# A four-layer decoder on one core: layer 0's expert output normalised inside the next attention, early router logits, ordered expert lists, a new pace of side work, and early loads for layer 2

## The chip, the cores and the metric

The kernel runs on one core of one Trainium2 chip. The metric is device time in microseconds for one execution of the whole decoder; less is better. Engines are named as in the profile: PE (matmuls), PEld (its weight loads), DVE, ACT, POOL, and SP, which issues most DMAs. L12 is line 12 of the kernel before.

## The reference, cut to what matters

The decoder works on x of 16 sequences × 100 positions × 128 features, with a context of 1444 × 96 for each sequence. Twelve sublayers follow one another, each added to x: four layers of attention, cross-attention and a feed-forward part. Those that the change touches compute:

```python
# layer 0, cross-attention: 16 heads over the 1444 context rows
# layer 0, feed-forward: the two best of 8 experts
probs = softmax(x @ gate_w.T + gate_b); w, idx = top_k(probs, 2); w = w / w.sum(-1)
y = sum over the two experts e of  w_e * (silu(x @ w1[e]) * (x @ w3[e])) @ w2[e]
# layer 1, attention: 16 heads of 8, weights quantised to 5 levels; softmax of masked scores
# layer 2, attention: batch norm, two softmaxes per head, difference, root mean square per head
att = softmax(q1 @ k1) - lam * softmax(q2 @ k2); y = rms_norm(att @ v) * (1 - lam0); x = x + y @ c
# layer 2, cross-attention: 16 heads over the context
# layer 3, cross-attention: softmax over the 32 largest scores only, then an S4D convolution and a small MLP
# layer 3, feed-forward: the two best of 8 experts, softmax over the two logits
```

Every sublayer normalises x over its 128 features first. All arithmetic of x is in f32.

## The kernel before, in words

x lies in SBUF as X, 100 partitions (positions) × 16 batch elements × 128 features. It is worked on in NG = 4 groups of four batch elements. Before a sublayer, each group's rows get statistics (`stats4`, L335: bn_stats and bn_aggr on DVE, the power −0.5 on POOL in `root`, L354 and L356), are normalised into XN (`norm4`, L345, four DVE operations at L348), and turned by PE into XT, features on partitions (four transposes in `ahead`, L332, copied out at L292). `ahead` is a generator with three steps of this kind (statistics and root, XN, turn), and `at_once` runs all three. Sublayers run `ahead` for the next one group by group where they can.

A scheduler sets the order of each engine's instructions from the program's order and its own estimates; instructions wrapped in `pin` or `keep_in_program_order` keep the order in which they are written.

**Layer 0's cross-attention** (`l0_xattn`) runs 64 units of a batch element and four heads, 12 context chunks each, on a step counter `d` from 0 to 11. Steps 7 and 10 advance `ahead` of the group that has just ended. **Layer 0's experts** (`moe`, L1519) begin with the router: `logits` (L1334) is a product per batch element into one PSUM tile and one DVE add; `exps`, `top2` and `share` follow on DVE. `route` then builds, for 32 tiles of 128 (token, expert) places, the lists of rows: one-hot tables r_th, r_tv (L1460), r_oh (L1463) and r_tw (L1501) on DVE, sums on PE, and at the end the integers r_ti (source rows, L1489) and r_di (destination rows, L1491). For each of the 32 tiles POOL gathers rows by an indirect DMA (L1554), PE turns them (L1559), makes two products of four 128×128 blocks each (L1575), DVE multiplies (L1579), PE makes the down product (L1585), ACT scales, and POOL scatters the rows to `yd` in HBM (L1589). Beside the tiles runs `side`: `s4d_rest`, which prepares the S4D kernel of layer 3 on DVE (its last twenty steps are a multiplication at L1874 and a reduction at L1875 each), and `quant`, which quantises layer 1's weights. Four steps of `side` are taken per tile. At the end both result rows are loaded back (yy), added to X (L1623), and with `follow` the groups are normalised and turned at once, all four, before layer 1's attention begins.

**The attention helper** (`attn`, L365) is shared. Its units are pipelined by hand over a loop: scores of unit i, the largest score on DVE (L414), the scores minus it on POOL (L415, 100×1600), the exponent on ACT (L419), transposes (L378, copied at L428), products with V, and row sums, up to eight units behind. POOL also makes kb for each unit (L388, 128×1600). `prep(g)` yields the projections of group g: group 0 runs ahead of the loop, the others one step per unit. A list `later` holds work of ended groups, advanced by one step per unit. `spread` (L486) makes the tile va and sets it to 1.0 on POOL (L489). **Layer 1's attention** has 16 units.

**Layer 2's attention** (`l2_attn`) has 32 units, two per batch element. Its `room` is a large tile of 12288 columns, of which 6400 hold queries and keys. When a group of four batch elements has ended, `ended(g)` goes to `later`: the square root on ACT (L721, with a table load), a reciprocal, four times o on POOL (L727), its transposes ps_ot, a copy on ACT (L734), the product ps_out and the addition to X (L740), then `ahead`: some 15 steps for a group. The list is chained, and what remains after the loop is run to its end. **Layer 2's cross-attention** (`l2_xattn`) loads its two weight tiles (L1122) and the context of batch elements 0 and 1 (L1136, L1137) through SP when it starts; its first matmuls are ps_q (from XT) and ps_k (from the context).

**Layer 3's thresholds** (`l3_means`) take, for each of 52 blocks of scores, the 32 largest of every row: maxima of segments (L1954), four rounds of max and replace (L1958, L1963) into `m8`, a slice of one tile `big` for all blocks, the mask wk on DVE (L1964), and its product with the exponents on POOL (L1971). At the end the 32nd largest of every block is read from `big`.

Of the kernel before, what the change touches and what calls it, by code (L numbers as in the profile page):

```python
# [221 lines left out]
class Decoder:  # L222
    def __init__(self, tc, ctx, ins, at, out):
# [45 lines left out]
        self.a_rs = cp.tile([S, B], F32, name="a_rs")  # L269
        self.bst = cp.tile([128, NG, 6], F32, name="bst")  # L270
# [95 lines left out]
    def attn(self, pools, units, halves, mode, finish, prep):  # L366
# [96 lines left out]
        for i in range(N + 8):  # L463
            at = lambda lag, step, *a: step(i - lag, *a) if 0 <= i - lag < N else None
            at(4, results)
            at(-1, masked)
            for g in range(4):
                at(0, scores, g)
                at(2, turned, g)
                if g == 0:  # L470
                    at(5, lambda j: next(fin[j], None))
                if g == 1:
                    at(6, lambda j: next(fin[j], None))
                    at(7, lambda j: next(fin[j], None))
                if g == 2:
                    at(1, numerators)
            at(0, maxima)
            at(3, values)
            at(4, lambda j: next(fin[j], None))
            if later:  # L480
                next(later[0], None)
            for p in preps[: i + 1]:
                next(p, None)
# [140 lines left out]
    def l1_attn(self):  # L624
        with ExitStack() as st:
# [5 lines left out]
            def prep(g):  # L631
                self.project(psT, g, self.w("l1_qkv", 0, 128), qT, None, 1.0 / math.sqrt(8.0))
# [6 lines left out]
    def l2_attn(self):  # L639
        nc = self.nc  # L640
        with ExitStack() as st:
# [7 lines left out]
            room = self.fw.tile([128, 12288], F32, tag="big", name="l2_qk")  # L649
            t = [room[:, j * NT : (j + 1) * NT] for j in range(4)]  # L650
# [303 lines left out]
    def l0_xattn(self):  # L954
# [9 lines left out]
        with ExitStack() as st:  # L964
# [101 lines left out]
            for s in range(NCH * (NU + 1) + LEAD + 6):  # L1066
# [23 lines left out]
                if d in (7, 10) and ahead:  # L1090
                    next(ahead[0] if d < 10 else ahead.pop(), None)
# [5 lines left out]
    def l2_xattn(self):  # L1097
# [13 lines left out]
        with ExitStack() as st:  # L1111
# [7 lines left out]
            def weights(tag, rows):  # L1119
                n = ins[tag].shape[-1]  # L1120
                t = xw.tile([rows, n], F32, name=f"{tag}_sb")
                nc.sync.dma_start(out=t, in_=ins[tag])  # L1122
                return lambda k: t[:, self.xat[tag][k][0] : sum(self.xat[tag][k])]
# [15 lines left out]
            fetch(0)  # L1139
            fetch(1)  # L1140
# [202 lines left out]

    def exps(self, lg, ne, w1):
# [62 lines left out]
    def route(self, sel, both, cmb, mc, w1, psM, psO):  # L1407
# [3 lines left out]
        nc = self.nc  # L1411
        ones = w1.tile([S, S], F32, name="ones")
# [25 lines left out]
        for j, v in enumerate((rk, cmb)):  # L1438
# [5 lines left out]
        nc.vector.tensor_scalar(hi, pos, 1.0 / 128.0, -127.0 / 256.0, ALU.mult, ALU.add)  # L1444
        nc.vector.tensor_scalar(hi, hi, RND, None, ALU.add)
        nc.vector.tensor_scalar(hi, hi, -RND, None, ALU.add)
        lo = w1.tile([S, 2 * B], F32, name="r_lo")
        nc.vector.scalar_tensor_tensor(lo, hi, -128.0, pos, ALU.mult, ALU.add)
        va = w1.tile([S, 2, 2 * B], F32, name="r_va")
        nc.vector.scalar_tensor_tensor(va[:, 0], hi, -2.0, mc("id64")[:S], ALU.mult, ALU.add)  # L1450
        nc.vector.tensor_tensor(va[:, 1], mc("id1")[:S], lo, ALU.subtract)
# [5 lines left out]
        nc.vector.tensor_tensor(th, mc("iota")[:S, :NTL].unsqueeze(1).to_broadcast([S, 2 * B, NTL]),  # L1457
                                hi.unsqueeze(2).to_broadcast([S, 2 * B, NTL]), ALU.is_equal)
        for j in range(2):
            nc.vector.tensor_tensor(tv[:, :, j], th, va[:, j].unsqueeze(2).to_broadcast([S, 2 * B, NTL]), ALU.mult)  # L1460
        pl = psO.tile([128, 512], F32, tag="po", name="ps_l")
        for i in range(0, 2 * B, 8):
            nc.vector.tensor_tensor(oh[:, i : i + 8], mc("iota")[:S].unsqueeze(1).to_broadcast([S, 8, 128]),  # L1463
                                    lo[:, i : i + 8].unsqueeze(2).to_broadcast([S, 8, 128]), ALU.is_equal)
# [17 lines left out]
        nc.vector.scalar_tensor_tensor(dst, lst[:, :NTL], 64.0, lst[:, NTL:], ALU.mult, ALU.add)  # L1482
        nc.vector.tensor_tensor(dst, dst, mc("own"), ALU.add)
        nc.vector.tensor_scalar(dst, dst, 0.0, 2.0 * NT + 128.0 * NTL - 1.0, ALU.max, ALU.min)
        tok = w1.tile([128, NTL], F32, name="r_tok")
        nc.vector.tensor_scalar(tok, dst, float(NT), -float(NT), ALU.is_ge, ALU.mult)
        nc.vector.tensor_tensor(tok, dst, tok, ALU.add)
        ti = w1.tile([128, NTL], I32, name="r_ti")
        nc.vector.tensor_scalar(ti, tok, NT - 1.0, None, ALU.min)  # L1489
        di = w1.tile([128, NTL], I32, name="r_di")  # L1490
        nc.vector.tensor_copy(di, dst)  # L1491

        def weights():
# [4 lines left out]
            for j in range(3):  # L1498
                nc.vector.tensor_copy(pb[:, j], cur)
                nc.vector.tensor_copy(pt[:, j], pb[:, j])  # L1500
                nc.vector.tensor_tensor(tw[:, :, j], th, pt[:, j].unsqueeze(2).to_broadcast([S, 2 * B, NTL]), ALU.mult)  # L1501
# [17 lines left out]
    def moe(self, wt, gw, bg, on_probs, follow, taps=False):  # L1519
# [4 lines left out]
        with ExitStack() as st:  # L1524
# [11 lines left out]
            lg = self.logits(gw, 8, bg, w1, psM)  # L1536
# [61 lines left out]
            for t in range(NTL):  # L1598
# [11 lines left out]
                for _ in range(4):  # L1610
# [4 lines left out]
            for g in range(NG):  # L1615
# [8 lines left out]
                if follow:  # L1624
                    self.at_once(g, psM)
# [252 lines left out]
    def l3_means(self, CT, odd, room, wqk, cq, aside=None):  # L1878
# [6 lines left out]
        with ExitStack() as st:  # L1885
# [21 lines left out]
            if fast:  # L1907
                big = xw.tile([128, NUN, 4, 8], F32, name="big")
# [37 lines left out]
            def candidates(s, ex, i):  # L1946
# [5 lines left out]
                m8 = big[:, i]  # L1952
# [11 lines left out]
                pin(nc.vector.tensor_scalar(wk, s, m8[:, 3, 7:8], None, ALU.is_ge))  # L1964
                yield wk, m8, nm
# [119 lines left out]
            if fast:  # L2085

                sure = xw.tile([128, NUN], F32, name="sure")
                nc.vector.tensor_scalar(sure, big[:, :, 3, 7], -0.5 * BIG, None, ALU.is_gt)
# [171 lines left out]
    def run(self, layers):  # L2260
# [4 lines left out]
        if 2 in layers:  # L2265
            self.moe(self.big("l0f"), self.w("l0_gw"), self.r("l0_bg"), True, True, taps=True)
# [16 lines left out]
        if 11 in layers:  # L2283
            self.moe(self.big("l3f"), self.w("l3_gw"), self.r("l3_bg"), False, False)
# [25 lines left out]
```

## Time and profile before

| | us |
|---|---|
| median of 3 runs | 4224.94 |
| lowest and highest | 4224.86, 4239.69 |
| the profiled execution | 4216.78 |
| its span in the profile | 4215.0 |
| PE, DVE, ACT, POOL busy | 3776.6 (90%), 2941.8 (70%), 2001.1 (47%), 1056.5 (25%) |
| layer 0's cross-attention ends, about | 1446 |
| first and last tile's POOL transfer of layer 0's experts | 1480.83, 1602.44 |
| first projection of layer 1's attention | 1631.68 |
| layer 2's attention: first units, last row sums | 2008, 2293 |
| first keys of layer 2's cross-attention (ps_k) | 2341.47 |
| layer 3's experts: logits, last matmuls of the tiles, about | 4070, 4173 |

Times inside the program are microseconds from the span's start. A row of groups reads: line, engine, operation, output<-input, shapes and count, then busy time and mean nanoseconds of one, then the idle time of the engine just before them and what ended it. A row of waits reads: waiting engine, tile and line, the releaser, then total, number and longest wait. The granted clock is TensorE's, 1.00 being full speed; over the whole execution it was 0.93.

### The profile page before, as it was taken

To read this page: it belongs to the slowest core of one execution; us is meant where nothing else is said; L and a number is where in the kernel's file an instruction comes from. 1 tells how busy PE (TensorE), PEld (TensorE's weight loads), DVE (VectorE), ACT (ScalarE), POOL (GpSimd) and SP (SyncE) were. 2 spreads that over 40 slices of the span, in tenths; PEclk is the share of its full clock that TensorE was granted. 3 is DMA by queue.
4 is the path that set the end of the run, shared out by engine and by line. 5 is a ranking of instruction groups with operands and counts; after the bars stand their busy time and mean duration, and the time that the engine had idled before them with its cause. 6 is when DMAs were issued, how large, how long until landed. Compare 5 with 4: busy or idle time off the path is not lost. (4 is left out here: it accounts for less than half of the span.)

```text
span 4215.0 us, 65293 instructions
## 1 busy us (share of the span) xinstructions
PE 3776.6 (90%) x24498; PEld 2419.7 (57%) x24498; DVE 2941.8 (70%) x7850; ACT 2001.1 (47%) x3941; POOL 1056.5 (25%) x755
## 2 busy tenths in 40 slices
PE   7899999999999877898998799999997978888658
PEld 4555555555555475574666365556665646666448
DVE  8677777777777775754675577666764678996744
ACT  3365666656666432332454254445453445665114
POOL 6400000000000055504785000000004445443125
PEclk9899999999999888999998799999998979998879
DMA  2200000000000010153000000000000011110012
GB/s 68 88 12 17 17 14 17 17 14 17 17 14 6 5 34 25 40 155 64 1 1 2 20 13 16 12 12 12 12 2 1 1 49 39 40 34 19 2 73 60
DMA packets 36883, 112.00 MB, mean 27 GB/s; under 512 B 4998, under 2 KB 19628, under 8 KB 35472
## 3 DMA queue, kind: packets, MB, share of 16 engines
q1 hardware_dynamic: 28786, 97.19, 8.0%
q0 software_dynamic: 4096, 8.40, 0.7%
q8 instruction: 197, 3.23, 0.3%
q10 hardware_dynamic: 3678, 2.16, 0.2%
q14 instruction: 126, 1.03, 0.1%
HBM read 100.97 MB, written 6.75 MB: 26 GB/s over the span
## 5 line engine op out<-in xcount | busy, mean ns | idle before, releaser
L971 PE MATMUL ps_s<-qk,ct 97*128 97x400 f32 (+1 forms) x1536 | 651.7, 507 | 0.7 <-DVE qk L999 0.7
L971 PE MATMUL ps_o<-st,cn 128*97 128x400 f32 (+1 forms) x1536 | 649.6, 505 | 0.0
L1216 DVE TENSOR_REDUCE pm<-ps_s 100x1 f32<-100x484 f32 (+1 forms) x768 | 469.0, 653 | 232.2 <-PE ps_s L1130 219.4
L1006 ACT COPY st<-ps_s 128x400 f32<-128x400 f32 (+1 forms) x768 | 375.8, 489 | 424.5 <-PE ps_s L971 421.6
L1251 ACT ACTIVATE pt<-ps_st 121x400 f32<-121x400 f32 (+1 forms) x768 | 343.9, 501 | 347.0 <-PE ps_s L1130 338.6
L1015 DVE TENSOR_TENSOR mx<-mx,st 128x400 f32<-128x400 f32 (+1 forms) x640 | 365.0, 570 | 165.4 <-ACT st L1006 163.1
L1130 PE MATMUL ps_s<-K,q 32*100 32x484 f32 (+1 forms) x1536 | 421.8, 630 | 1.7 <-DVE pm L1216 1.6
L1036 DVE TENSOR_TENSOR st<-st,nb 128x400 f32<-128x400 f32 (+1 forms) x768 | 402.9, 566 | 8.6 <-ACT nb L1032 2.5
L971 PEld LDWEIGHTS ps_s<-qk,ct 97*128 97x128 f32 (+1 forms) x1536 | 267.0, 184 | 233.5 <-issue 92.2
L1037 ACT ACTIVATE st<-st 128x400 f32<-128x400 f32 (+1 forms) x768 | 378.0, 535 | 42.3 <-DVE st L1036 41.9
L1130 PE MATMUL ps_st<-q,K 32*121 32x300 f32 (+3 forms) x3072 | 380.3, 365 | 0.6 <-ACT pt L1251 0.6
L971 PEld LDWEIGHTS ps_o<-st,cn 128*97 128x97 f32 (+1 forms) x1536 | 237.2, 163 | 233.6 <-issue 142.8
L1025 POOL TENSOR_TENSOR nd<-cst_sb,nm 100x400 f32<-100x400 f32 x64 | 54.7, 854 | 1139.8 <-DVE nm L1023 1139.8
L1130 PEld LDWEIGHTS ps_st<-q,K 32*121 32x121 f32 (+1 forms) x3072 | 272.4, 182 | 47.5 <-issue 4.8
L354 POOL TENSOR_SCALAR a_rs<-a_mv 100x4 f32<-100x4 f32 x60 | 14.0, 234 | 980.4 <-DVE a_mv L340 973.0
L378 PEld LDWEIGHTS ps_pt<-cst_sb,sc 100*100 100x100 f32 x1280 | 138.8, 131 | 135.1 <-issue 88.7
L1937 PE MATMUL ps_s<-ct,qk 97*128 97x512 f32 (+3 forms) x384 | 173.8, 668 | 46.5 <-ACT sc L1943 36.1
L2015 PEld LDWEIGHTS ps_m<-rw,l3x_ex 128*128 128x128 f32 (+1 forms) x1536 | 192.7, 203 | 37.4 <-POOL rw L2007 27.0
L1971 POOL TENSOR_TENSOR l3x_ex<-l3x_ex,wk 128x1444 f32<-128x1444 f32 x52 | 168.6, 3243 | 179.3 <-DVE wk L1964 91.8
L2015 PE MATMUL ps_m<-rw,l3x_ex 128*128 128x100 f32 (+1 forms) x1536 | 198.7, 288 | 16.5 <-POOL rw L2007 16.3
L415 POOL TENSOR_TENSOR sc<-sc,mx 100x1600 f32<-100x1600 f32 x64 | 183.2, 2863 | 107.8 <-DVE mx L414 82.3
L1954 DVE MAX8 cd<-sc 128x8 f32<-128x45 f32 (+1 forms) x1664 | 182.4, 189 | 22.0 <-ACT sc L1943 21.9
(538 smaller groups left out, 7057.4 us busy)
## 6 DMA issues: line engine op xcount, KB each, us to landing
ct<-in_ctxT SPq DMA_DIRECT2D x64, 541.5 KB
cn<-in_ctxn SPq DMA_DIRECT2D x48, 582.0 KB
wb<-gd SPq DMA_DIRECT2D x8, 800.0 KB
l0f_sb<-in_l0f SPq DMA_DIRECT2D x3, 2048.0 KB
l3f_sb<-in_l3f SPq DMA_DIRECT2D x3, 2048.0 KB
wts_sb<-in_wts SPq DMA_DIRECT2D x1, 2320.0 KB
l0x_raw<-in_l0x SPq DMA_DIRECT2D x1, 1800.0 KB
l1f_sb<-in_l1f SPq DMA_DIRECT2D x1, 1728.0 KB
```

What stands on the lines that cost most here:

```text
L415: pin(nc.gpsimd.tensor_tensor(scs[i], scs[i], mx.unsqueeze(2).to_broadcast([S, NH, S]), ALU.subtract))
L971: mm = lambda *a, **k: tc.keep_in_program_order(nc.tensor.matmul(*a, **k))
L1006: nc.scalar.copy(t[:n], ps[:n, :G4])
L1015: nc.vector.tensor_tensor(MX[u][:n], MX[u][:n], t[:n], ALU.max)
L1036: nc.vector.tensor_tensor(t[:n], t[:n], NM[u][:n], ALU.subtract)
L1037: nc.scalar.activation(t[:n], t[:n], AF.Exp)
L1130: mm = lambda *a, **k: tc.keep_in_program_order(nc.tensor.matmul(*a, **k))
L1216: nc.vector.tensor_reduce(pm[:, a, r // 32, n : n + 1], ps[:S, : n1 - n0], AX.X, ALU.max)
L1251: nc.scalar.activation(pt[: n1 - n0, r // 32, :], ps[: n1 - n0, :G4], AF.Exp)
L1937: nc.tensor.matmul(o, lhsT=q, rhs=ctx[bb][:, n0:n1], start=True, stop=True)
L1954: pin(nc.vector.max(cd[:, k, :], s[:, n0:n1]))
L2015: nc.tensor.matmul(acc[b][:, c // 4, (c % 4) * S : (c % 4 + 1) * S], lhsT=ex[r0:r1, c * 128 : (c + 1) * 128], rhs=rw[r0:r1], start=first a ...
```

## The change

Seven edits. (1) `moe` no longer normalises and turns its output: `prep(g)` of layer 1's attention does it, in its first two steps. (2) The router's logits are made per group by a new `logits4` into a tile that lives through the program; in layer 0 groups 0 to 2 are done inside the cross-attention, in a step `d == 11` to which the turn of `ahead` moves from step 10; `moe` does the rest (`known` groups are left out). Layer 3 makes all four in `moe`. (3) In `route`, the DVE instructions from r_hi to r_di, with r_tw, are pinned in program order, in both expert layers. (4) `side` gets two steps per tile. (5) `later` gets two steps per unit. (6) `l2_attn` issues the loads of layer 2's cross-attention weights and of the context of batch elements 0 and 1 into the unused columns of `room`. (7) In `l3_means`, `m8` is a rotating tile, and its last column is copied by POOL into a small tile `last`, once for each of 52 blocks.

```diff
 # attn
-            if later:
-                next(later[0], None)
+            for p in later[:1] * 2:
+                next(p, None)
...
 # l1_attn
             def prep(g):
+                steps = self.ahead(g, psT)
+                next(steps)
+                yield
+                next(steps)
+                next(steps, None)
+                yield
                 self.project(psT, g, self.w("l1_qkv", 0, 128), qT, None, 1.0 / math.sqrt(8.0))
...
 # l2_attn
             room = self.fw.tile([128, 12288], F32, tag="big", name="l2_qk")
+            self.early, p = {}, 4 * NT
+            for tag, rows in (("l2x", 128), ("l2xk", CA), (0, CA), (1, CA)):
+                n = CK if tag in (0, 1) else self.ins[tag].shape[-1]
+                e = self.early[tag] = room[:rows, p : p + n]
+                nc.sync.dma_start(out=e, in_=self.ins["ctxT"][tag] if tag in (0, 1) else self.ins[tag])
+                p += n
...
 # l0_xattn
                 if d in (7, 10) and ahead:
-                    next(ahead[0] if d < 10 else ahead.pop(), None)
+                    next(ahead[0], None)
+                if d == 11 and ahead and 0 <= v < NU - 1:
+                    next(ahead.pop(), None)
+                    self.logits4(v // (4 * NQ), self.w("l0_gw"), self.r("l0_bg"), psA)
...
 # l2_xattn
-                t = xw.tile([rows, n], F32, name=f"{tag}_sb")
-                nc.sync.dma_start(out=t, in_=ins[tag])
+                t = self.early[tag]
...
-            fetch(0)
-            fetch(1)
+            cts.update({b: self.early[b] for b in range(2)})
...
+    def logits4(self, g, gw, bias, psp):
+        ps = psp.tile([128, 512], F32, tag="ps", name="ps_lg")
+        for j in range(4):
+            b = 4 * g + j
+            self.nc.tensor.matmul(ps[:S, 8 * j : 8 * j + 8], lhsT=self.XT[:, b * S : (b + 1) * S], rhs=gw,
+                                  start=True, stop=True)
+        self.nc.vector.tensor_tensor(self.lg[:, 4 * g : 4 * g + 4, :], ps[:S, :32].rearrange("p (b e) -> p b e", e=8),
+                                     bias.unsqueeze(1).to_broadcast([S, 4, 8]), ALU.add)
...
 # route: pin(...) around each DVE instruction from r_hi to r_di, r_tw among them
-                nc.vector.tensor_tensor(tw[:, :, j], th, pt[:, j].unsqueeze(2).to_broadcast([S, 2 * B, NTL]), ALU.mult)
+                pin(nc.vector.tensor_tensor(tw[:, :, j], th, pt[:, j].unsqueeze(2).to_broadcast([S, 2 * B, NTL]), ALU.mult))
...
 # moe
-            lg = self.logits(gw, 8, bg, w1, psM)
+            for g in range(known, NG):
+                self.logits4(g, gw, bg, psM)
+            lg = self.lg
...
-                for _ in range(4):
+                for _ in range(2):
                     next(side, None)
...
-                if follow:
-                    self.at_once(g, psM)
...
 # l3_means
-                big = xw.tile([128, NUN, 4, 8], F32, name="big")
+                last = xw.tile([128, NUN], F32, name="last")
...
-                m8 = big[:, i]
+                m8 = wp.tile([128, 4, 8], F32, tag="m8", name="m8")
...
                 pin(nc.vector.tensor_scalar(wk, s, m8[:, 3, 7:8], None, ALU.is_ge))
+                nc.gpsimd.tensor_copy(last[:, i : i + 1], m8[:, 3, 7:8])
...
-                nc.vector.tensor_scalar(sure, big[:, :, 3, 7], -0.5 * BIG, None, ALU.is_gt)
+                nc.vector.tensor_scalar(sure, last, -0.5 * BIG, None, ALU.is_gt)
```

## The prediction

> **What bounds the kernel now.** I read the page's engine shares first: PE is busy 90% of a 4215.0 us span, so a gain can come only from stretches where PE waits, and anything added where PE is full is paid. Then I tabled busy time by stretch around the steps that the change touches.
>
> ```profile
> 1510.00:1517.00 7.00, 4.96 (x29) 4.56 (x29) 7.00 (x12) 1.58 (x3) 4.07 (x4) 0.77 0.16 47
> ...
> 1531.00:1538.00 7.00, 4.46 (x28) 4.30 (x27) 7.00 (x12) 1.58 (x3) 0.98 (x1) 0.76 0.03 11
> ...
> 1545.00:1600.00 55.00, 54.09 (x485) 53.85 (x484) 27.81 (x75) 27.59 (x56) 32.45 (x33) 1.00 0.17 40
> 1600.00:1632.00 32.00, 6.57 (x29) 4.45 (x29) 15.35 (x59) 1.72 (x4) 9.86 (x11) 0.59 0.22 60
> ```
>
> The columns are the stretch, its length, then PE, weight loads, DVE, ACT, POOL busy with counts, the granted clock, DMA share and GB/s. In layer 0's expert tiles (first two rows) DVE is full, 7.00 of 7, and PE is not; from 1545 on PE is full and DVE half idle. From 1600 to 1632 nothing is full: layer 0's experts end and layer 1's attention starts.
>
> ```profile
> 2040.00:2200.00 160.00, 158.66 (x1445) 111.77 (x1445) 110.17 (x176) 86.64 (x148) 124.88 (x64) 1.00 0.01 1
> 2200.00:2220.00 20.00, 16.00 (x124) 11.05 (x123) 14.71 (x16) 6.93 (x11) 12.04 (x6) 0.75 0.01 2
> ...
> 2296.00:2341.00 45.00, 16.86 (x64) 12.49 (x64) 13.07 (x51) 5.47 (x13) 10.49 (x20) 0.53 0.12 33
> ```
>
> Layer 2's attention keeps PE full until its units end near 2296; then 45 us with PE busy 16.86. What PE waits for there, from the waits view of 2296 to 2342:
>
> ```profile
> PE ps_turn L332 <- DVE XN L348: 14.0, 3, 6.3
> PE ps_k L1130 <- DMA ct<-in_ctxT: 7.4, 1, 7.4
> PE ps_ot L378 <- POOL o L727: 5.4, 2, 3.5
> PE ps_out L377 <- ACT ot L734: 3.8, 8, 0.5
> ```
>
> The rest of group 1's and all of groups 2's and 3's finishing work run one after another, then the next attention waits for its context.
>
> **The change, term by term.** Sums are differences to the profiled execution (4216.78 us, 1.78 above its span).
>
> Side work at two steps a tile. Its 20 kernel steps are one L1874 and one L1875 each; their groups between 1509.7 and 1545.1 read:
>
> ```profile
> L1875 DVE TENSOR_REDUCE kern<-pr 128x5 f32<-128x640 f32 x19 | 14.6, 801 | 0.0
> L1874 DVE TENSOR_TENSOR pr<-bt,gt 128x640 f32<-128x640 f32 x18 | 14.0, 807 | 0.0
> ```
>
> Start to start a step takes about 1.465 us; four a tile are 5.86, and the tile's own three DVE operations (xT, wb, h) take 1.13, so a tile takes 7.0 against 2.79 undisturbed. The down matmuls start at 1509.70 and, eight tiles later, at 1554.86: 45.16 − 8×2.79 = 22.8 us lost. In the changed DVE order eight steps fall within the first eight kernel tiles, at most 1.13 + 1.465 = 2.6 < 2.79 a tile on average: hidden under PE. Six tiles carry two: 1.13 + 2.93 = 4.06, so 6×1.27 = 7.6 us stay. Two bounds: if idles of 1.27 us lower the granted clock, three bursts of eight matmuls take 1.92 each as in the disturbed tiles, 5.9 a tile, 18.7 lost, gain 4; if not, gain 15.2. An idle of 0.91 in this stage left the bursts at 1.06, idles from 1.86 gave 1.92; 1.27 is nearer the first. I take **−13** (−15 to −4). The Trainium skill, "TensorE: Matmul & The Clock Gate", section "Why this matters for your kernels", asks only that no PE gap exceed about 3 us; by it the clock would never fall here and the term would be −15.2. The rows speak against it: no single wait in these tiles is above 2.8 us and the clock is 0.76.
>
> Early logits. Three groups of eight 8-column matmuls go into layer 0's cross-attention, where PE is busy 300.00 of 300 between 1100 and 1400. The 24 took 2.26 us at 1446.89, under the last group's norm (XN at 1450.45): they were hidden, now they are paid. **+2.3** (0 to +4, if the turn moved one step later costs a stall). The last group's chain stays; layer 3 keeps its 32 matmuls in the same place and its four small adds are hidden by them but the last.
>
> Ordered lists. DVE now does all of r_tv, r_oh and all three r_tw before r_ti. One r_tw of 1.22 us comes ahead of r_ti in both expert layers, so the first gather (POOL, 3.26 us, directly on the chain) starts about 0.9 later; in exchange PE has the r_wg matmuls, 13 + 3 + 1 + 15 in layer 0, done before the first tile instead of between its matmuls, about 0.9 each time less 0.5. **+1** for both (−0.5 to +2.5).
>
> Norm and turn in layer 1's attention. Before, all four groups' norms and sixteen turns stand on PE ahead of the first projection (1631.68), and POOL's 2.34 us memset comes late (1624.13). After: the eight additions of X (last load lands about 1614.5), the memset, group 0's root, XN near 1621, projection near 1623.3, and POOL builds kb near 1627 rather than
>
> ```profile
> 1635.41 5.68 POOL L388 TENSOR_TENSOR kb<-kT,cst_sb 128x1600 f32<-128x1600 f32 x2 [6.57 <-DVE kT L292]
> 1643.80 2.86 POOL L415 TENSOR_TENSOR sc<-sc,mx 100x1600 f32<-100x1600 f32 x1 [2.71 <-DVE mx L414]
> ```
>
> Not all 8 us survive: in POOL's new order four kb (2.86 each) and a root stand before the first sc, so sc starts near 1639.5 instead of 1643.80, and the next ones gain as much or more (1649.44 was behind a kb). The XN of groups 1 to 3 now run beside kb. I take **−6** (−11 to +1).
>
> Layer 2's attention. Group 1's last steps and all of group 2's move into the units. In the drain they took 2296.2 to 2318.66, 22.5 us, of which group 3 still needs the table load and square root, 2.0. The wait for the context, 2333.72 (XT) to 2341.47, 7.7, goes since the four loads are issued when the attention starts (SP idles there; 26 GB/s over the span). Gross −28.2. In the units, PE then has two turns (0.93 each), four ps_ot (0.39) and four ps_out (0.6): 5.8 on a full PE; one more pair of table loads, which cost 1.34 of PE in the stretches holding them (18.66 of 20); and an XN stall, seen once:
>
> ```profile
> 2202.81 0.41 DVE L709 TENSOR_REDUCE ss<-sq 100x16 f32<-100x256 f32 x1
> 2203.14 6.71 DVE L348 TENSOR_SCALAR XN<-X,a_mv,a_rs 100x128 f32<-100x128 f32 x4
> ...
> 2203.57 2.86 POOL L415 TENSOR_TENSOR sc<-sc,mx 100x1600 f32<-100x1600 f32 x1
> 2206.39 2.86 POOL L388 TENSOR_TENSOR kb<-l_qk,cst_sb 128x1600 f32<-128x1600 f32 x1
> ```
>
> Four XN take 6.71 us here and 1.11 at 1616.04, where POOL is idle; behind them the copies that PE waits for cost it 4.0 us. Group 0 pays this before and after; group 1 pays it newly, group 2's XN comes after the last kb and sc. Sum 5.8 + 1.3 + 4.0 = 11.1, less about 1 for the units' thin end (PE 13.34 of 20 after 2280): +10. Net **−18** (−28, everything hidden, to −8, with a stall of 4 for every moved table load and XN). The Trainium skill, "SBUF — State Buffer", section "Who interferes with whom", speaks against this part of the change: VectorE's scalar forms and GpSimd share a port pair as an exclusive lock, and the later one blocks for the whole instruction. By that rule alone each moved XN could wait out one POOL operation of 2.86, 11.4 a group. The trace shows 5.6 more for four, of which 4.0 reach PE; the sum has the 4.0.
>
> Copies in layer 3's thresholds. 52 POOL copies of one column; no row has that form. Nearest are 0.18 (memset 100x100) and 0.23 (tensor_scalar 100x4). Each stands ahead of L1971, which waits for wk (0.97 us after the copy's source), so it ends under wk: 0. If each instead holds wk back by its own 0.2, DVE being nearly full there, +10. DVE's wk starts 0.03 us after the last maximum, ahead of any signal to POOL: I take **0** (0 to +10).
>
> Sum: −13 + 2.3 + 1 − 6 − 18 + 0 = −33.7. On the profiled execution that is 4183; the runs' median is 4224.94, 8.2 higher, and the forecast is on that scale: 4224.9 − 33.7 = **4191**.
>
> **Rivals.**
> Layer 2 gives nothing. Two steps a unit crowd one unit: a table pair, an XN stall and two output pairs fall on a PE with 1.34 idle in 160, and the gain of 28 returns as stalls. For it: 4.0 lost at 2206 from one XN group. Against: the drain is 45 us and the moved PE work 5.8. Then −15.7: 4209.
> The clock stays low in the experts and the attention's start is POOL-bound. For it: clock 0.76 wherever DVE leaves gaps, four kb before sc. Then −4 + 2.3 + 1 + 0 − 18 = −18.7: 4206.
> Slower: copies and wk block each other. One wk took 2.339 us against a median of 0.973, +1.37. If that befalls each of 52, +71, so 4191 + 71 = 4262; it cancels the gain from 0.65 us a copy on, and makes the kernel slower by over 0.5% from 1.05. Against: the copy is 1444 times narrower than what POOL runs there, and ready while POOL mostly idles.
>
> **How the numbers follow.** Forecast (4177 to 4203) 0.65; layer 2 gives nothing 0.15; clock and POOL 0.15; slower 0.05. The terms' bounds together reach −54.5 to +5.5; taken as independent, eight in ten lie within about 15 of the sum, and the two middle rivals lie inside a range of **4175 to 4211**. This kernel's measurement can tell 0.5%, 21 us, from no change: faster means below 4203.8. All of the forecast but 0.02, and 0.1 of the two middle rivals, lie below it: faster 0.73, same 0.22, slower 0.05.
>
> **What would show it.** Right: in the profile after, down matmuls of layer 0 never more than about 4.1 apart; the first projection of layer 1 near 10 us after the last load; no wait for a context at layer 2's first keys, and about 18 us rather than 45 between the last unit and them, with units about 10 us longer in all; wk's median still 0.97. Wrong: a granted clock of 0.75 over the six two-step tiles; PE waits of 4 us per group at L428 in more than two places; wk above 1.1; a first scaling of scores (L415) no earlier than before.

## The result and the profile after

The changed kernel is slower. Median 4240.13 us over 18 runs (4222.03 to 4249.7) against 4222.98 us for the kernel before over 18 runs (4206.14 to 4239.69): ratio 1.0035, 95% interval 1.002 to 1.005. The forecast was 4191, range 4175 to 4211, a gain of about 0.8%. The loss of 0.35% lies outside the range and on the other side, though it is less than the 0.5% that the text on record held for a clear difference.

The profiled execution of the changed kernel took 4249.7 us (span 4247.9), the one of before 4216.78: 33 us apart, twice the difference of the medians. The two are therefore compared stretch by stretch, and a stretch counts only where the other profiles below repeat it.

| stretch, us | before | after | difference | on record |
|---|---|---|---|---|
| start to the first scores of layer 0's cross-attention | 192.6 | 198.7 | +6.1 | – |
| layer 0's cross-attention | 1254.2 | 1256.3 | +2.1 | +2.3 |
| its end to the first expert multiplication | 45.0 | 43.9 | −1.2 | about +0.5 |
| first to 32nd expert multiplication | 107.8 | 93.6 | −14.3 | −13 |
| last scatter to the 16th scaling of layer 1's attention | 154.4 | 161.0 | +6.6 | −6 |
| layer 2's attention, first kb to last y | 286.1 | 318.2 | +32.2 | +10 |
| last y to the first ps_k of the cross-attention | 46.9 | 18.7 | −28.2 | −28.2 |
| first ps_k to first ps_O | 61.9 | 77.1 | +15.2 | 0 |
| first to last ps_O | 783.5 | 788.4 | +4.9 | 0 |
| thresholds of layer 3, first to 52nd wk | 438.8 | 448.6 | +9.8 | 0 |

The first row and the last are not the change's: the same instructions of the start took 190.4 to 198.7 us in the fourteen profiles, those of the thresholds 434.7 to 448.9, with no order by edit; the granted clock there ranges from 0.88 to 0.95 and from 0.88 to 0.92. The row from the first to the last ps_O ranges from 781.8 to 788.5 in the same way. The row of layer 1's attention is not steady either: f2_sideonly, below, which leaves layer 1 as it was, takes 149.7 us there against 154.4 before, with the same first scaling (40.5 us and 40.4 after the last scatter) and a clock of 1.00 rather than 0.94 in its last part.

Busy time by stretch in the changed kernel (stretch, length, PE, weight loads, DVE, ACT, POOL, clock, DMA share, GB/s) at the places shown of before:

```profile
1510.00:1517.00 7.00, 7.00 (x65) 7.00 (x64) 6.71 (x25) 3.74 (x9) 5.00 (x6) 1.00 0.17 49
...
1531.00:1538.00 7.00, 7.00 (x65) 7.00 (x64) 6.49 (x14) 3.69 (x8) 5.22 (x6) 1.00 0.19 50
...
1545.00:1600.00 55.00, 43.85 (x370) 41.56 (x369) 37.88 (x84) 22.22 (x44) 26.68 (x25) 0.98 0.16 38
1600.00:1632.00 32.00, 9.69 (x28) 5.62 (x28) 23.51 (x59) 2.27 (x3) 15.84 (x12) 0.61 0.17 45
```

In the expert tiles PE is full where DVE was, and at full clock. In layer 2's attention the opposite has happened:

```profile
2040.00:2200.00 160.00, 145.02 (x1281) 103.82 (x1280) 101.92 (x159) 80.18 (x134) 112.14 (x59) 0.94 0.01 2
2200.00:2328.00 128.00, 113.19 (x1028) 82.69 (x1027) 76.67 (x139) 59.19 (x100) 76.36 (x47) 0.92 0.00 1
2328.00:2345.00 17.00, 8.41 (x33) 6.50 (x34) 5.30 (x20) 2.15 (x6) 7.10 (x11) 0.52 0.26 66
```

PE was busy 158.66 of the first 160 us before, and is busy 145.02 now, with the clock down to 0.94. The waits view of 2040 to 2330 says for what:

```profile
PE ps_ot L379 <- POOL o L741: 17.6, 4, 4.8
PE ps_turn L333 <- DVE XN L349: 12.8, 4, 4.1
PE ps_pt L379 <- ACT pt L429: 1.3, 2, 0.6
```

The first two waits are new inside the units: three of 4.27 us for o (the fourth, of 4.8, stands behind the last y) and two pairs of 4.1 and 2.3 for XN, 25.6 us in all. In the kernel before all of PE's waits there, from 2040 to 2298, come to 8.0, of which 4.0 for copies of pt behind XN. What is left of the 32 goes with the lower clock; how much of it does was not measured apart. One of each in order of time; PE, then POOL at the same place:

```profile
2111.52 1.56 PE L378 MATMUL ps_pv<-pt,va 100*32 100x300 f32 x32
2117.35 0.59 PE L379 MATMUL ps_ot<-cst_sb,o 100*128 100x100 f32 x2 [4.27 <-POOL o L741]
```

```profile
2108.99 2.87 POOL L389 TENSOR_TENSOR kb<-l_qk,cst_sb 128x1600 f32<-128x1600 f32 x1
2113.85 2.86 POOL L416 TENSOR_TENSOR sc<-sc,mx 100x1600 f32<-100x1600 f32 x1 [1.99 <-DVE mx L415]
2116.67 1.20 POOL L741 TENSOR_TENSOR o<-va,ss 100x256 f32<-100x256 f32 x2
```

The step that makes the first o and the step whose transposes read it stand in one unit. POOL reaches o only behind the unit's own scaling of scores, which waits for the largest score; PE, whose order is written, cannot pass the transposes to the row sums behind them. The brackets give it: 4.27 us of idle PE, released by POOL's o. The second pair:

```profile
2158.34 1.56 PE L378 MATMUL ps_pv<-pt,va 100*32 100x300 f32 x32
2164.01 0.40 PE L333 MATMUL ps_turn<-cst_sb,XN 100*128 100x100 f32 x1 [4.11 <-DVE XN L349]
2166.74 0.94 PE L333 MATMUL ps_turn<-cst_sb,XN 100*128 100x100 f32 x3 [2.33 <-DVE XN L349]
```

XN itself was slow there, beside POOL; DVE, then POOL:

```profile
2160.87 6.33 DVE L349 TENSOR_SCALAR XN<-X,a_mv,a_rs 100x128 f32<-100x128 f32 x4
```

```profile
2160.92 2.86 POOL L416 TENSOR_TENSOR sc<-sc,mx 100x1600 f32<-100x1600 f32 x1
2163.74 2.86 POOL L389 TENSOR_TENSOR kb<-l_qk,cst_sb 128x1600 f32<-128x1600 f32 x1
```

### The profile page after: what moved, and what is told of

It is laid out like the page before. It is cut to its first block, busy times and chain, and to the rows that moved or that the text cites. A ratio compares the mean times of both kernels' runs of the same rounds, so it can differ in the third digit from the quotient of the medians.

```text
span 4247.9 us, 65343 instructions
## 1 busy us (share of the span) xinstructions
PE 3810.7 (90%) x24498; PEld 2440.3 (57%) x24498; DVE 2961.5 (70%) x7856; ACT 2004.6 (47%) x3943; POOL 1070.0 (25%) x807
## 5 line engine op out<-in xcount | busy, mean ns | idle before, releaser
L379 PE MATMUL ps_pt<-cst_sb,sc 100*100 100x100 f32 x1280 | 167.4, 255 | 21.4 <-ACT sc L420 10.0
```

Source lines behind the costliest of these rows:

```text
L379: turn = lambda o, i: pin(nc.tensor.transpose(o, i, self.ident[: i.shape[0], : i.shape[0]]))
```

## The experiments

Runs of one group shared a chip with runs of the kernel before; its medians were 4223.2, 4234.0, 4230.8 and 4223.0 us in the four groups, so ratios are compared across groups and times only within one. In the second and third groups the expert tiles ran slower: layer 3's tiles, whose work no edit changes, took 90.1 to 94.2 us there from the first to the last multiplication, and 84.5 to 86.0 in the other profiles. Why is not shown; the chip alone is not, since the second and the fourth group carry the same chip number and have 91.2 to 91.3 and 84.6.

**First group: which edit costs what.** The theory T1 was that two steps that depend on each other in one unit are the cause; the rival R1, that the moved work itself is.

e1_later1:

```diff
-            for p in later[:1] * 2:
+            for p in later[:1]:
```

> The changed kernel with one step of the ended groups' work per unit again (edit 5 undone), the rest kept. In the changed profile the stretch from layer 2's first kb to its last y is 318.2 us (286.1 before) and from there to the first ps_k 18.7 (46.9 before). Theory T1: two steps that depend on each other now stand in one unit, PE keeps its written order and waits at their head (17.6 us for o, 12.8 for XN), with a lower clock behind. Then one step a unit brings the first stretch back to 286 to 289, and the second to about 39 (46.9 less the wait for the context of 7.7): together 325 to 328 against 336.9, so 9 to 12 us faster than the changed kernel. Rival R1: the units grow by the amount of work that is moved into them, wherever its steps stand, and by POOL's port: group 1's last steps and group 2's leave the units, 11 us by the working on record, so 307 and 39, together 346, 9 us slower than the changed kernel.

4209.77 us, ratio 0.9969 (0.9949 to 0.9988). The stretches are 284.3 and 40.5, together 324.8: T1's size, and R1's 346 is out. In time the kernel gains more than the expected 9 to 12 us: the ratios differ by 0.66%, some 28 us. The two stretches give 12 of them, and 16 lie in the stretch that follows (60.7 us from the first ps_k to the first ps_O, 77.1 in the changed kernel), which the expectation had not reckoned with.

e2_spaced, in `ended`:

```diff
                         now = o.rearrange("p h e -> p (h e)")
+                    if b == 4 * g:
+                        yield
+                        yield
...
-                yield from self.ahead(g, psT, pin=pin)
+                steps = self.ahead(g, psT, pin=pin)
+                next(steps)
+                yield
+                next(steps)
+                yield
+                yield
+                for _ in steps:
+                    pass
                 yield
```

> The changed kernel, still two steps a unit, but with empty steps put into the ended groups' work, so that the first o is made a unit ahead of its transposes on PE, and XN a unit ahead of the turn. T1: the waits of 17.6 and 12.8 us nearly vanish; the first stretch (first kb to last y of layer 2) falls from 318.2 to 294 to 300 (286.1 plus the moved PE work of 5.8, a table pair and one XN stall), the second stays at 19 to 24: 17 to 24 us faster than the changed kernel. R1: the work is the same, so the first stretch stays within 4 of 318 and the time within noise of the changed kernel.

4205.62 us, ratio 0.9948 (0.9926 to 0.9971). The first stretch is 288.1, below what T1 had allowed; the second 20.6. All the moved work is still in the units, and they grow by 2 us, not by 32. Against the changed kernel the ratios differ by 0.87%, some 37 us, where 17 to 24 were expected: 28 come from these two stretches together, and 4 from the next one (72.8). Waits of PE from 2040 to 2300:

```profile
PE ps_so L378 <- ACT os L445: 4.0, 3, 1.3
PE ps_turn L333 <- DVE XN L349: 3.6, 1, 3.6
PE ps_out L378 <- ACT ot L751: 3.5, 7, 0.5
PE ps_pt L379 <- DVE pt L429: 2.3, 2, 1.5
PE ps_ot L379 <- POOL o L741: 1.8, 1, 1.8
```

and the two stretches of its units:

```profile
2040.00:2200.00 160.00, 155.41 (x1443) 109.92 (x1436) 109.67 (x178) 89.07 (x150) 128.00 (x67) 1.00 0.01 1
2200.00:2288.00 88.00, 81.39 (x799) 59.00 (x797) 53.60 (x106) 46.28 (x78) 56.36 (x37) 1.00 0.00 1
```

The waits for o and XN that remain stand after the last unit, at 2290 and 2293. T1 holds, in both directions.

e3_atonce:

```diff
 # l1_attn, prep
-                steps = self.ahead(g, psT)
-                next(steps)
-                yield
-                next(steps)
-                next(steps, None)
-                yield
 # moe, after the additions of yy
+                if taps:
+                    self.at_once(g, psM)
```

> The changed kernel with edit 1 undone: the four groups are normalised and turned at once before layer 1's attention. From the last scatter of layer 0's experts to the sixteenth scaling of scores (L415 in the kernel before) the changed profile has 161.0 us, the kernel before 154.4. Theory T2: XN beside POOL's kb blocks DVE (5.96, 2.98 and 5.67 us for six XN that take 0.34 each alone), and a kb that waits for a buffer stands ahead of the first scaling, so the earlier first projection is lost again: then 154 to 156 here, 5 to 7 us faster than the changed kernel. Rival: the loss comes from the lower clock there or from what the later side work leaves over; then it stays within 2 of 161.

4230.73 us, ratio 1.0011 (0.9994 to 1.0029). The stretch is 153.1 us, 8 below the changed kernel. Undoing edit 1 pays; where XN stands, c2_norms asks.

e4_nocopy:

```diff
                 last = xw.tile([128, NUN], F32, name="last")
+                nc.gpsimd.memset(last, 0.0)
...
-                nc.gpsimd.tensor_copy(last[:, i : i + 1], m8[:, 3, 7:8])
```

> The changed kernel without the 52 copies of one column on POOL: the tile last is set to zero once instead, so the test of the 32nd largest value against the mark for masked keys is left out. From the first to the 52nd mask wk the changed profile has 448.6 us, the kernel before 438.8. Theory T3: the 9.8 us are clock and the time at which context arrives, no wait for the copies (the usual distance of 8.1 between two masks is unchanged, only single distances are 1.5 to 2.5 longer): then this stretch differs from run to run by such amounts, and here it may be anything from 438 to 449; the time is within noise of the changed kernel. Rival: the copies hold up POOL's queue where the context's mask is made; then it is 439 and the kernel about 10 us faster than the changed one.

4239.85 us, ratio 1.0037 (1.0021 to 1.0052), the changed kernel's own. The stretch is 441.4, inside the spread of kernels that have the copies. In the changed profile a copy took 179 to 922 ns, median 185, and wk's median is 978 ns against 973: no cost is seen.

**Second group: mending the rest.** c1_best is e2_spaced and e3_atonce together with another pace:

```diff
-                for _ in range(2):
+                for _ in range(4 if t < 5 else 1 if t < 25 else 2):
                     next(side, None)
```

> The spaced steps of e2_spaced, layer 1's groups normalised and turned at once as in e3_atonce, and the side work paced 4 steps a tile for five tiles, 1 for twenty, 2 for the rest, so that no tile carries two kernel steps of 2.93 us before the last ones. By the term sums: e2 took 34 us off the changed kernel, e3 9; the six tiles of 4.06 to 4.36 in the changed profile lost 8.1 us, of which all but two tiles' 2.6 should go, so the experts' 93.5 us from first to last multiplication become 86 to 89. Median 4188 to 4194, about 0.8% under the kernel before. Rival: side work at one step a tile comes too late and is left over after the last tile (two kernel steps and the quantising stand in the last six tiles): then the experts' stretch gains nothing and the median is near 4197.

4213.23 us, ratio 0.994 (0.992 to 0.9961): less than expected. In this group the stretch of the tiles was 98.0, where c4_xnonly, with the old pace, had 101.1; the pace is worth 3 us there (c2_norms and c3_warm, with the same pace, have 96.0 and 94.7). In g2_all, with tiles at full rate, it was 87.6 against 93.5, within the expected 86 to 89.

c2_norms takes the groups' norms out of the steps, and leaves the turn there:

```diff
             vs, (va,) = self.spread(pools)
+            turns = [self.ahead(g, psT) for g in range(NG)]
+            for p in turns:
+                next(p)
+            for p in turns:
+                next(p)
...
-                steps = self.ahead(g, psT)
-                next(steps)
-                yield
-                next(steps)
-                next(steps, None)
+                next(turns[g], None)
                 yield
```

> As c1_best, but layer 1's four groups are normalised before the attention begins, ahead of every kb on POOL, and only the turn stands in the attention's steps. T2 says that the earlier first projection was lost to XN beside kb: without that the stretch from the last scatter to the sixteenth scaling is 146 to 151 (153.1 in e3_atonce, 161.0 in the changed kernel), and the median some 3 to 7 us below c1_best. Rival: the attention's first units are bound by what each group's steps add to PE and DVE, wherever XN stands: then it stays at 157 to 161 and the kernel is 4 to 8 us slower than c1_best.

4210.19 us, ratio 0.9943 (0.992 to 0.9965). The stretch is 148.3 us: 5.6 below c1_best's 154.0, and within what T2 asked. By itself that is weak, since f2_sideonly has 149.7 with the norms where they were; the steadier sign is the first scaling of scores, which starts 43.6 us after the last scatter in the changed kernel (42.4 to 43.9 in all seven with XN in the steps), 40.1 to 40.7 in the five that normalise at once, and 35.6 to 35.9 in c2_norms and g2_all. In the changed kernel DVE shows what the place of XN costs; its rows in order of time:

```profile
1619.95 5.96 DVE L349 TENSOR_SCALAR XN<-X,a_mv,a_rs 100x128 f32<-100x128 f32 x3
...
1628.53 2.98 DVE L349 TENSOR_SCALAR XN<-X,a_mv,a_rs 100x128 f32<-100x128 f32 x1 [1.02 <-POOL a_rs L357]
...
1639.88 5.67 DVE L349 TENSOR_SCALAR XN<-X,a_mv,a_rs 100x128 f32<-100x128 f32 x2
```

and POOL beside them:

```profile
1620.14 5.68 POOL L389 TENSOR_TENSOR kb<-kT,cst_sb 128x1600 f32<-128x1600 f32 x2 [1.32 <-ACT kT L293]
...
1628.57 2.86 POOL L389 TENSOR_TENSOR kb<-kT,cst_sb 128x1600 f32<-128x1600 f32 x1
1636.97 2.86 POOL L389 TENSOR_TENSOR kb<-kT,cst_sb 128x1600 f32<-128x1600 f32 x1 [5.54 <-PE ps_s L378]
1639.79 5.68 POOL L416 TENSOR_TENSOR sc<-sc,mx 100x1600 f32<-100x1600 f32 x2
```

Six XN took 14.6 us beside kb and sc. In c2_norms seven of them take 1.86, before any kb, and POOL reaches the first scaling at 1628.69:

```profile
1611.07 1.86 DVE L349 TENSOR_SCALAR XN<-X,a_mv,a_rs 100x128 f32<-100x128 f32 x7
```

c3_warm is c1_best with this, called in group 3's finishing work (28 before the first ps_ot, 2 behind each, 16 before the turn):

```diff
+            def busy(n):
+                ps = psT.tile([128, 512], F32, tag="ps", name="ps_busy")
+                for _ in range(n):
+                    pin(nc.tensor.transpose(ps[:, :S], self.ident[:S, :128], self.ident[:S, :S]))
```

> As c1_best, with 52 more transposes of a constant on PE, written to PSUM and never read, in the waits of group 3's finishing work after layer 2's last unit. From the first ps_k to the first ps_O of layer 2's cross-attention there are 61.9 us in the kernel before, 77.1 in the changed one and 72.8 in e2_spaced, with the granted clock at one half for 12, 35 and 50 us after the first ps_k. Theory T4: the half clock there is what PE's idleness in the finishing work leaves behind: with PE kept busy the clock stays at full speed and the stretch falls to 44 to 52; the finishing work itself grows by 0 to 3. Rival: the half clock follows the attention's end whatever PE does then (its start stood 2.1 to 4.3 us after the last y in every profile): the stretch stays at 60 to 77, and the kernel is no faster than c1_best.

4205.84 us, ratio 0.9923 (0.9896 to 0.995). The stretch is 71.1: the 44 to 52 that T4 asked for do not come. But T4 was not fully put to the test, because PE was not kept busy to the end: the last transposes end at 2301.4, PE then waits 2.43 us for XN and 1.01 before the first ps_k at 2306.4, and the clock is 1.00 from 2304 to 2305 and 0.50 from 2306 on. The windows show it up while the transposes run and low behind them:

```profile
2295.00:2305.00 10.00, 6.50 (x53) 5.17 (x51) 3.74 (x16) 1.33 (x5) 3.82 (x9) 1.00 0.41 108
2305.00:2315.00 10.00, 8.26 (x22) 2.36 (x24) 2.86 (x6) 1.70 (x4) 3.46 (x1) 0.51 0.02 5
2315.00:2325.00 10.00, 9.35 (x26) 2.18 (x26) 4.54 (x9) 1.57 (x3) 0.00 (x0) 0.50 0.00 0
```

c4_xnonly is the changed kernel with the second part of e2_spaced's diff alone.

> The changed kernel with empty steps between XN and the turn alone; the first o and its transposes stay in one unit. T1 prices the two pairs by PE's waits in the changed profile: 17.6 us for o (four groups), 12.8 for XN. Then the stretch from layer 2's first kb to its last y falls from 318.2 to 303 to 308 (288.1 with both spaced), and PE's wait for o stays near 17. Rival: the two pairs are not separate, a unit that is late by one lets the next pair wait no more: then it is either near 290 or near 318.

4242.29 us, ratio 1.0014 (0.9996 to 1.0031). The stretch is 314.3, 4 below the changed kernel's: the price of 303 to 308 was wrong, and the rival's 318 is nearer. Its waits say why:

```profile
PE ps_ot L379 <- POOL o L741: 17.6, 4, 4.8
PE ps_pt L379 <- DVE pt L429: 7.2, 2, 3.6
```

The wait for XN at the turn is gone, but DVE is still held by XN, and PE now waits for the copies of pt behind it. So with XN spaced, spacing o as well is worth 26 us of the 30 that both bring; o alone was not run.

**Third group: the stretch after.**

f1_lateload puts the loads of edit 6 back to where they were (`fetch(0)`, `fetch(1)` and the two weight loads in `l2_xattn`), in e2_spaced.

> e2_spaced with edit 6 undone: the weights and the first two contexts of layer 2's cross-attention are loaded when it starts, as in the kernel before. The stretch from layer 2's last y to the first ps_k was 46.9 us before, 18.7 in the changed kernel and 20.6 in e2_spaced; without the early loads it should be about 28 (the wait for the context, 7.7 us, returns). What is asked is the next stretch, from the first ps_k to the first ps_O: 61.9 in the kernel before and 60.7 in e1_later1, 72.8 in e2_spaced, 77.1 in the changed kernel, with the clock at one half for longer. Theory T5: the wait for the context is what let the clock return sooner in the kernel before, so the early loads' gain is given back in the clock: then 60 to 63 here, and the sum of both stretches 88 to 91 against 93.4 in e2_spaced. Rival: the wait and the clock have nothing to do with each other (e1_later1 had neither the wait nor the slow clock): then 71 to 77 here, and the kernel is 7 to 8 us slower than e2_spaced.

4213.38 us, ratio 0.9953 (0.9929 to 0.9976). The stretches are 27.2 and 71.1: the wait for the context is back (7.6), the longer head stays. T5 falls; 98.3 against 93.4, so by these profiles the early loads are worth about 5. The ratios differ by 2 us only, inside their intervals, where 7 to 8 were expected.

f2_sideonly, the kernel before with edit 4 alone:

```diff
-                for _ in range(4):
+                for _ in range(2):
                     next(side, None)
```

> The kernel before with one edit alone, two steps of side work per tile rather than four (edit 4). In the changed kernel the stretch from the first to the last multiplication of layer 0's experts fell from 107.8 to 93.6. If that is edit 4's doing, as the working on record says (22.8 us lost, 7.6 left), it falls here by 13 to 15 as well and the kernel is 13 to 15 us faster than before, a ratio of 0.9965 to 0.997. Rival: part of it came from the ordered lists or the earlier logits; then it falls by less than 11.

4216.18 us, ratio 0.9964 (0.9948 to 0.998), as expected. In its profile the stretch fell only to 99.3, by 8.5, which the rival had asked for; but layer 3's tiles took 94.2 there rather than 86.0. The six tiles with two steps stand as in the changed kernel (their multiplications 4.05 to 4.06 us apart in both), and what is missing lies in other tiles, 3.4 to 5.0 apart where the changed kernel has 2.8. The timed ratio, with the kernel before on the same chip, says 15 us, from 8 to 22 by its interval; it takes in whatever layer 1's attention gained (149.7 against 154.4 in the profiles), so it does not give the tiles' share alone.

**Fourth group.** g1_rest, in e2_spaced:

```diff
-                pin(nc.vector.reciprocal(ss[:, bs, :], ss[:, bs, :]))
+                for _ in range(37 if g == NG - 1 else 1):
+                    pin(nc.vector.reciprocal(ss[:, bs, :], ss[:, bs, :]))
```

> e2_spaced with 36 more reciprocals on DVE in group 3's finishing work (an even number, 0.55 us each, so the values come back), that is about 20 us in which PE rests before layer 2's cross-attention; nothing is moved. Every kernel so far with one step per unit has 40 to 47 us between layer 2's last y and the first ps_k, and then 60.7 to 62.2 from there to the first ps_O; every kernel with two steps has 18.7 to 27.2, and then 71.1 to 77.1, with the clock at one half for longer. Theory T6: the clock comes back sooner after a longer rest, so that a shorter finishing stretch is given back in the next one: here 40 to 41, then 60 to 63. Rival: the length of the rest has no bearing, and something in the units decides it: here 40 to 41, then 70 to 77, and the kernel is 20 us slower than e2_spaced.

4219.47 us, ratio 0.9988 (0.9966 to 1.001). The stretches are 41.7 and 67.4: neither T6's 60 to 63 nor the rival's 70 to 77. A longer rest gave back 5.4 us of the head. The clock did come up at once (0.58, 1.00 and 0.94 in the first three stretches of 10 us from the first ps_k, 0.50 in all three in e2_spaced), but fell to 0.50 for the next 40. So the length of the rest bears on when the clock comes up, and doesn't explain the whole difference.

g2_all is c2_norms with the transposes of c3_warm.

> c2_norms with the 52 transposes of c3_warm in group 3's finishing work, the fastest parts of all runs together. c2_norms had 0.9943 of the kernel before, c3_warm 0.9923. In c3_warm the clock was at full speed in the finishing work for 10 us, but at one half from the first ps_k on, so the gain there is small: 0 to 3 us. Expected: 0.991 to 0.994 of the kernel before, the stretch from the last scatter of layer 0's experts to the sixteenth scaling 148 as in c2_norms. Rival: the transposes cost their own time in the drain, 1 to 3 us slower than c2_norms.

4187.45 us, ratio 0.9902 (0.9876 to 0.9928), the fastest of all; the median is better than the expected 0.991 to 0.994, though the interval reaches into it. By its profile the transposes are not why: from last y to first ps_k it has 22.0, and then 77.1, where c2_norms has 20.6 and 74.6. What it has over e2_spaced is in the expert tiles (87.6 against 93.5) and in the start of layer 1's attention (149.2 against 161.0).

## Why the prediction was wrong, point by point

The early logits (+2.3) measured +2.1. The ordered lists (+1 for both heads) measured −1.2 in layer 0's head and +1.1 in layer 3's (38.5 us before, 39.6 after, from the first logits to the first multiplication), nothing in sum. The side work (−13) measured −14.3: the down products of six tiles stand 4.07 to 4.36 us apart, near the 4.06 worked out, and the clock stayed at 0.98 over them; f2_sideonly, with this edit alone, is 8 to 22 us faster. The drain and the context (−28.2) measured −28.2. The copies (0) cost nothing that could be seen.

The step that failed is the price of the units: "In the units, PE then has two turns (0.93 each), four ps_ot (0.39) and four ps_out (0.6): 5.8 on a full PE", with 1.3 for a table pair and 4.0 for an XN stall, +10 in sum. The units grew by 32. The work itself was priced too high, if anything: with the steps spaced it costs 2 (e2_spaced). What was missing is the wait that the edit adds: two steps a unit put a producer and its consumer into one unit, and PE's order is written, so everything behind the consumer waits. The prediction counted instructions, with one XN stall of 4.0 taken from the copies behind XN, and put the wait of the second step of a unit for the first at nothing. It held a crowded unit for a rival worth 0.15, but as crowding, with the gain of 28 returned; the actual price was 32, of which 25.6 in waits of 2.3 to 4.3 us, with the lower clock behind them. The sign that it named, waits of 4 us at the copies of pt (L428), did not appear; the waits stood at ps_ot and ps_turn.

The junction (−6, measured +6.6 against this profile) failed at "The XN of groups 1 to 3 now run beside kb", which was written down and priced at nothing. POOL's order came as forecast, two kb, a root and two kb ahead of the first sc; but that sc starts 43.6 us after the last scatter, where the forecast's 1639.5 is 36.1 after it and the kernel before has 40.4; no earlier first scaling was one of the signs of being wrong on record. Six XN cost 14.6 us on DVE, among the first scores' copies, and the fourth kb waits 5.54 for its buffer ahead of the first sc. e3_atonce and c2_norms have stretches 8 and 12.7 shorter. The rows of 5.96, 2.98 and 5.67 us stand beside POOL's 2.86 and 5.68. The Trainium skill, "SBUF — State Buffer", section "Who interferes with whom", says that a scalar operation of VectorE can enter a mode with two ports, and that it and a GpSimd operation then block each other for the whole instruction. The rows agree with it; the prediction had cited the page against layer 2 only. c2_norms, which moves the statistics, their roots and XN ahead of every kb and leaves the turn, brings the first scaling forward by 7.7 us; how much of that is XN's slowness and how much the order on POOL was not parted.

The third part was not in the sum at all: after layer 2's attention the next 60 us of work run longer, 71.1 to 77.1 in every kernel whose units take two steps (67.4 in g1_rest), 60.7 to 62.2 in every kernel that takes one. So of the 28 us that the drain gave, 15 were given back in the changed kernel, with the clock at one half for longer. That it goes with edit 5 is shown by e1_later1, which undoes this edit alone. The wait for the context is not the cause (f1_lateload), and the length of the rest is a part of it (g1_rest, 5.4 of some 11). An idle PE in the finishing work does not tell the kernels apart: e1_later1 has more of it than the changed kernel (40.5 us of finishing work against 18.7), and both have the same waits of 3.9 and 1.0 us just before the first ps_k. Whether a PE kept busy to the end would keep the clock up is open, since c3_warm left 3.4 us of waits. What the rest of the cause is stays open.

Taken together, +22 over the record in the units, +15 in the head and +13 at the junction make 50, and −33.7 plus 50 is +16, near the 17 between the medians. That it comes so near is in part luck: the rows are from single profiles, and the junction's alone varies by 5 us between the kernel before and f2_sideonly, which have the same code there.

## What to carry to other kernels

When work is interleaved in steps, the distance between a step and the one that needs it is part of the schedule: doubling the steps per unit halves it, and on an engine whose order is written down the consumer then blocks all that follows. Before moving an operation, look at what runs on the other engines at the new place, DVE's scalar forms beside POOL's long ones above all. And a saving in a stretch with a lowered clock should be followed into the next stretch before it is booked.

## What the runs showed of the hardware

The granted clock can stay at one half on a PE that hardly rests. In the changed kernel, from 2350 to 2360 PE is busy 9.35 of 10 us and from 2360 to 2380 18.88 of 20, at 0.50; the kernel before came up to full speed at 2353, 12 us after its first ps_k. After, then before:

```profile
2350.00:2360.00 10.00, 9.35 (x26) 2.30 (x22) 4.74 (x8) 1.50 (x4) 0.00 (x0) 0.50 0.00 0
2360.00:2380.00 20.00, 18.88 (x63) 7.90 (x59) 9.50 (x17) 3.22 (x7) 0.00 (x0) 0.50 0.00 0
```

```profile
2341.00:2353.00 12.00, 10.80 (x24) 2.85 (x24) 3.54 (x7) 1.69 (x3) 3.10 (x1) 0.50 0.01 4
2353.00:2364.00 11.00, 9.79 (x49) 3.95 (x48) 7.81 (x15) 3.09 (x6) 0.00 (x0) 0.98 0.00 0
```

The Trainium skill, "TensorE: Matmul & The Clock Gate", section "What's actually happening", gives about 3.4 us of sustained work as enough for full speed. Here 9 us without a gap in the profile's rows were not (2347.53 to 2357.09; the gaps around are 0.7 us at most), and the measurement decides. The pattern is not chance: the stretch from the first ps_k to the first ps_O is 77.10 to 77.11 us in the changed kernel, e3_atonce, e4_nocopy, c4_xnonly and g2_all, 72.82 in both e2_spaced and c1_best, and 71.11 in both c3_warm and f1_lateload. And four XN, 1.11 us together where POOL idles, took 6.33 beside two POOL operations of 2.86 in the units of layer 2, and three took 5.96 at the start of layer 1.
